# A head's exponentials laid together in DRAM: rows read back in pieces of 2048 bytes instead of four of 512

## The chip, the core and the metric

The kernel runs on one core of a Trainium2 chip. The core has a matrix engine (TensorE, PE in the profile; its weight loads are PEld), three engines for elementwise work (VectorE or DVE, ScalarE or ACT, GpSimd or POOL), and a queue that issues DMAs (SyncE, SP). They run side by side and wait for one another through semaphores. DMAs issued by SP run on the core's 16 DMA engines. The metric is the device time of one execution in microseconds; the median of the runs counts.

## What is computed

There are 64 graphs of 256 nodes with 512 features. Each goes through two layers, the first with two graph attentions. A graph attention projects the features, makes two logits per node and head, and weighs neighbours by a softmax over the sum of the logits of the two ends. Cut to its core, the reference is:

```python
def gat_layer(x, mask, W, a_src, a_dst, bias, concat):
    xl = (x @ W).reshape(B, N, H, F)
    asrc = jnp.einsum('bnhf,hf->bnh', xl, a_src)
    adst = jnp.einsum('bnhf,hf->bnh', xl, a_dst)
    e = jax.nn.leaky_relu(asrc[:, :, None, :] + adst[:, None, :, :], 0.2)
    e = jnp.where(mask[..., None], e, NEG_INF)
    attn = jax.nn.softmax(e, axis=1)
    out = jnp.einsum('bsdh,bshf->bdhf', attn, xl)
    return out + bias                 # concatenated over heads, or their mean

h = relu(layernorm(x))
x = x + gat(elu(gat(h, 4 heads of 256)), 1 head of 512)
h = relu(layernorm(x))
x = x + relu(attention of 8 heads of 64 over h, softmax along the other axis)
```

The attention weights are thus a 256 x 256 matrix for each of 4 + 1 + 8 = 13 heads of a graph. An entry is the exponential of a leaky rectifier of a sum, so it can be had from exponentials of the single logits: apart from a factor that the softmax divides away, it is a maximum of two values, one of which is a product of a node's value and the other node's.

## The kernel before

**Work of a head.** Nodes stand on 128 partitions in T = 2 halves. `exps` (L284 and L481) makes exponentials of the logits for all nodes. One of them, w, is needed as a row: all 256 values of a head, on every partition. `spread` (from L233) does this by way of DRAM. A vector transpose (L237) turns the 128 x 32 tile w, whose columns are (head, half), in blocks of 32 x 32; after it, partition 32 j + c holds the values of column c for the 32 nodes of block j. A DMA (L239) writes this 128 x 32 tile, 16 KB, to `kept` in DRAM. Then one DMA for two heads (L244) reads `kept` back to all 128 partitions at once, into `bc`. Each such read waits for the landing of the write. The columns of two heads lie side by side in a block, so that a partition's row comes as four pieces, one for each block j, of 128 floats (512 bytes); for the single head of the second attention they are 256 bytes. `bc` is thus ordered (block, column, node in block), and `rows` holds views of it, one for each head, in the order (half, block, node in block).

`weigh` (L286 to L290) makes 128 x 256 entries of the weights: ACT multiplies the row by a per-partition value (L289, tile wy), and DVE takes the maximum with another per-partition value and applies the mask (L290, tile e). TensorE then uses e as weights: gat1 (L394), gat2 (L448), gat3 (L500).

**Calls of spread.** `rows1` (4 heads, two reads), `rows2` (1 head, one read) and `rows3` (8 heads, four reads) stand in the step lists. For the last graph rows2 and rows3 are left out, and `spread_at_once` makes the rows with TensorE (L253) in PSUM. `bc2` has four buffers, `bc1` one.

**The projections** are products by blocks with seven multiplications for eight (class Product, L54), whose sums of operands POOL makes (`left`, L215 to L218) and whose results ACT (`kept`, L60) and DVE (`put`, L260) take from PSUM.

**Another tile through DRAM.** The normalised features h of the next graph are written to DRAM and read back rearranged (`away`, L203 and L204), 512 KB each way, and transposed by DVE (`back`, L209) before POOL makes the sums.

**Order.** The whole program is unrolled, in an order written by hand: a head for the first graphs, `order` repeated for each r from 1 to 63, and a tail. Each item of these lists issues its instructions on all engines, and each engine works through its own in order. In `order`, work on three successive graphs is interleaved: the second layer's last attention of graph r-2, the second and third attention of r-1, the first of r, and the first projection of r+1. In one round the row reads come as follows: `1 away1`, later `-1 rows3`, `0 rows2`, then `1 rows1` near the end, followed by `-1 edges3 6` and two products. The next round begins with the last `edges3` and gat3 of r-2 and with edges2; then come edges1 0 and edges1 1, which are the first users of the rows of rows1. On SP, after rows1's reads, follow the two transposing DMAs of `cap3` (L373), the load of the next graph's x and adjacency (L301 and L303), the store of an output (L517), and the next write and read of h.

Of the kernel before, what the change touches and what calls it, by code (L numbers as in the profile page):

```python
# [8 lines left out]
F32 = mybir.dt.float32  # L9
BF16 = mybir.dt.bfloat16  # L10
I32 = mybir.dt.int32
AF = mybir.ActivationFunctionType
# [5 lines left out]
P = 128  # L18
# [14 lines left out]
def rows_of(ap: bass.AP, n: int) -> bass.AP:  # L33

    return bass.AP(tensor=ap.tensor, offset=ap.offset, ap=[[0, P], [1, n]])
# [62 lines left out]
def short_path(ctx, tc, flags, x, adj, w1, att_src1, att_dst1, b1, w2, att_src2, att_dst2, b2, w_proj, w_att,  # L98
               b_att, out):

    nc = tc.nc
    B, N, D = x.shape
# [5 lines left out]
    T = N // P  # L108
# [8 lines left out]
    work = ctx.enter_context(tc.tile_pool(name="work", bufs=2))  # L117
    small = ctx.enter_context(tc.tile_pool(name="small", bufs=4))
    dram = ctx.enter_context(tc.tile_pool(name="dram", bufs=4, space=DRAM))
# [113 lines left out]
    def spread(w, heads):  # L233


        wt = small.tile([P, 32], F32, name="wt")
        nc.vector.transpose(wt, w)  # L237
        kept = dram.tile([4, 32, 32], F32, name=f"kept{heads}")
        nc.sync.dma_start(kept.rearrange("j c i -> (j c) i"), wt)  # L239
        rows = []  # L240
        for h in range(0, heads, 2):
            k = min(2, heads)
            bc = work.tile([P, 4, T * k, 32], F32, name=f"bc{k}", bufs=3 * k - 2)
            nc.sync.dma_start(bc.rearrange("p j c i -> p j (c i)"),  # L244
                              kept[:, T * h:T * (h + k), :].rearrange("j c i -> j (c i)")[None].to_broadcast([P, 4, 32 * T * k]))
            rows += [bc[:, :, T * i:T * (i + 1), :].rearrange("p j t i -> p t j i") for i in range(k)]
        return rows

    def spread_at_once(w, h):

        pm = ps_mm.tile([P, 512], F32, name="pm")
        for t in range(T):
            nc.tensor.matmul(pm[:, t * P:(t + 1) * P], w[:, h, t:t + 1].to_broadcast([P, P]), ident, start=True, stop=True)  # L253
        return pm[:, :N].rearrange("p (t j i) -> p t j i", t=T, j=4)

    def total(dst, pm, add):
        if add is None:
# [28 lines left out]
    def weigh(dst, bc, xw, yw, mask, op):  # L286

        wy = work.tile([P, N], F32, name="wy", bufs=3)
        nc.scalar.activation(wy.rearrange("p (t j i) -> p t j i", t=T, j=4), bc, AF.Copy, scale=yw)  # L289
        nc.vector.scalar_tensor_tensor(dst, wy, xw, mask, ALU.max, op)  # L290

    class Graph:
# [87 lines left out]
        def rows1(self):  # L380
            self.bc1 = spread(self.w[0], H1)

        def edges1(self, h):
            e = self.e[1, h] = work.tile([P, T, N], F32, name="e", bufs=9)
            for s in range(T):
                weigh(e[:, s, :], self.bc1[h], self.ex1[:, h, s:s + 1], self.ex1[:, H1 + h, s:s + 1],
                      self.mask[:, s, :], ALU.mult)
# [42 lines left out]
        def rows2(self):  # L430
            self.bc2 = None if self.b == B - 1 else spread(self.w[1], 1)

        def edges2(self):
            e = self.e[2] = work.tile([P, T, N], F32, name="e", bufs=9)
            bc = self.bc2[0] if self.bc2 else spread_at_once(self.w[1][:, :T].rearrange("p (h t) -> p h t", t=T), 0)
            for s in range(T):
                weigh(e[:, s, :], bc, self.ex2[:, 0, s:s + 1], self.ex2[:, 1, s:s + 1],
                      self.mask[:, s, :], ALU.mult)
# [44 lines left out]
        def rows3(self):  # L483
            self.bc3 = None if self.b == B - 1 else spread(self.w[2], H3)

        def edges3(self, h):
            e = self.e[3, h] = work.tile([P, T, N], F32, name="e", bufs=9)
            bc = self.bc3[h] if self.bc3 else spread_at_once(self.w3, h)
            for s in range(T):
                weigh(e[:, s, :], bc, self.ex3[:, 0, h, s:s + 1], self.ex3[:, 1, h, s:s + 1],  # L490
                      self.cap[:, s, :], ALU.min)
# [20 lines left out]
        def range(self):  # L512
            nc.vector.tensor_reduce(ends[:, 0, self.b:self.b + 1], self.exs, AX.X, ALU.max)
            nc.vector.tensor_reduce(ends[:, 1, self.b:self.b + 1], self.exs, AX.X, ALU.min)
# [434 lines left out]
```

## Time and profile before

| what | value |
|---|---|
| median of 3 runs | 3214.87 us (3212.22 to 3218.14) |
| profiled execution, its own time | 3217.47 us |
| span of the profiled execution, first to last instruction | 3215.8 us |
| mean granted TensorE clock | 0.993 |
| packets of all DMAs | 439,843, 281.49 MB |
| row reads bc<-kept of two heads | 380 of 256 KB, 5.6 us median from issue to landing |
| row reads bc<-kept of one head | 63 of 128 KB, 4.8 us |
| writes kept<-wt | 190 of 16 KB, 1.4 us |
| write of h, read of h | 63 each of 512 KB, 3.2 and 3.6 us |
| DMA queue q1 (all DMAs of SP) | 31.8% of 16 engines' span |
| ACT, L289, wy<-bc | 1646 recorded, 498 ns each |
| ACT's idle time that ended with a landing of bc | 115.5 us in 50 waits |

How to read it: shares of busy time are of the whole span, and a busy matmul is not proof that TensorE is at its peak, because the ends of matmuls are modelled. A bracket at the end of a timeline line gives the idle time of that engine ahead of the group and what ended it. An engine's wait costs something only if the engine that sets the end comes to wait for it. In the stretches, each row holds the length, the busy time of PE, PEld, DVE, ACT and POOL with the number of instructions, then the granted clock, the DMA engines' busy share and the GB/s.

### The profile page before, as it was taken

To read this page: it belongs to the slowest core of one execution; us is meant where nothing else is said; L and a number is where in the kernel's file an instruction comes from. 1 tells how busy PE (TensorE), PEld (TensorE's weight loads), DVE (VectorE), ACT (ScalarE), POOL (GpSimd) and SP (SyncE) were. 2 spreads that over 40 slices of the span, in tenths; PEclk is the share of its full clock that TensorE was granted. 3 is DMA by queue.
4 is the path that set the end of the run, shared out by engine and by line. 5 is a ranking of instruction groups with operands and counts; after the bars stand their busy time and mean duration, and the time that the engine had idled before them with its cause. 6 is when DMAs were issued, how large, how long until landed. Compare 5 with 4: busy or idle time off the path is not lost. (4 is left out here: it accounts for less than half of the span.)

```text
span 3215.8 us, 60905 instructions
## 1 busy us (share of the span) xinstructions
PE 3136.3 (98%) x21808; PEld 2677.7 (83%) x21808; DVE 2285.2 (71%) x6379; ACT 1917.8 (60%) x4867; POOL 1178.1 (37%) x1434
## 2 busy tenths in 40 slices
PE   5899999999999999999999999999999999999997
PEld 3788888888888888888888888888888888888886
DVE  7667677677677677676676776776776776776765
ACT  2456556656666665665565566566566666655654
POOL 2343343343433433433433433434434334334332
PEclk8999999999999999999999999999999999999999
DMA  4233333333333333333333333332333333333331
GB/s 143 57 94 84 90 88 89 84 90 87 88 90 89 88 86 85 96 80 90 97 81 89 88 91 84 91 93 82 92 87 89 88 92 88 84 86 96 81 90 35
DMA packets 439843, 281.49 MB, mean 88 GB/s; under 512 B 109169, under 2 KB 389745, under 8 KB 439537
## 3 DMA queue, kind: packets, MB, share of 16 engines
q1 hardware_dynamic: 438160, 275.43, 31.8%
q8 instruction: 177, 2.90, 0.4%
q10 hardware_dynamic: 1376, 2.10, 0.2%
q14 instruction: 130, 1.06, 0.1%
HBM read 199.36 MB, written 69.70 MB: 84 GB/s over the span
## 5 line engine op out<-in xcount | busy, mean ns | idle before, releaser
L289 ACT ACTIVATE wy<-bc,exs_sb 128x256 f32<-128x256 f32 x1646 | 706.8, 498 | 168.3 <-DMA bc<-kept 115.5
L260 DVE TENSOR_TENSOR xl<-pm,kept 128x256 f32<-128x256 f32 (+2 forms) x768 | 321.7, 419 | 285.8 <-PE pm L54 206.8
L510 POOL TENSOR_TENSOR x<-x,o 128x256 f32<-128x256 f32 x256 | 180.9, 728 | 916.8 <-DVE r L506 885.6
L290 DVE SCALAR_TENSOR_TENSOR e<-wy,exs_sb,cap 128x256 f32<-128x256 f32 x1024 | 435.9, 478 | 92.1 <-ACT wy L289 92.1
L394 PE MATMUL pm<-xl,e 128*128 128x257 f32 x2048 | 488.5, 386 | 12.1 <-DVE e L290 9.1
L54 PE MATMUL sum<-w_sb,h1s 128*128 128x257 f32 x2048 | 489.2, 381 | 5.9 <-POOL h1s L216 3.4
L60 ACT ACTIVATE kept<-sum 128x264 f32<-128x264 f32 (+3 forms) x768 | 276.5, 376 | 338.2 <-PE sum L54 333.1
L54 PEld LDWEIGHTS sum<-w_sb,h1s 128*128 128x128 f32 x2048 | 389.9, 191 | 64.6 <-POOL h1s L216 3.8
L394 PEld LDWEIGHTS pm<-xl,e 128*128 128x128 f32 x2048 | 374.6, 190 | 76.5 <-issue 11.2
L54 PE MATMUL pm<-w_sb,h1s 128*128 128x257 f32 x1536 | 372.2, 385 | 14.9 <-DVE xl L260 10.7
L54 PEld LDWEIGHTS pm<-w_sb,h1s 128*128 128x128 f32 x1536 | 287.9, 191 | 79.4 <-POOL hs L216 21.2
L181 POOL TENSOR_TENSOR rstd<-ve,neg_half 128x2 f32<-128x2 f32 x128 | 117.7, 919 | 636.8 <-DVE ve L179 636.8
L500 PEld LDWEIGHTS pm<-xl,e 128*64 128x64 f32 x8192 | 250.5, 138 | 45.2 <-DVE e L290 23.6
L54 PE MATMUL sum<-w1a_sb,hs 128*128 128x260 f32 x1024 | 270.5, 387 | 11.5 <-ACT kept L60 4.9
L54 PE MATMUL sum<-w1b_sb,hs 128*128 128x256 f32 x1024 | 271.6, 388 | 4.1 <-DVE w1b_sb L536 2.1
L290 DVE SCALAR_TENSOR_TENSOR e<-wy,exs_sb,mask 128x256 f32<-128x256 f32 x640 | 270.3, 481 | 6.3 <-ACT wy L289 6.1
L54 PE MATMUL sum<-wp_sb,hs 128*128 128x264 f32 x1024 | 271.2, 388 | 1.1 <-ACT kept L60 1.1
L500 PE MATMUL pm<-xl,e 128*64 128x65 f32 x8192 | 269.6, 224 | 2.0 <-DVE e L290 1.3
L407 ACT ACTIVATE ez<-z 128x512 f32<-128x512 f32 x256 | 159.6, 624 | 178.2 <-DVE z L404 178.2
L404 DVE SCALAR_TENSOR_TENSOR z<-pm,r,b_sb 128x256 f32<-128x256 f32 x512 | 247.8, 484 | 18.3
L448 PE MATMUL pm<-xl,e 128*128 128x257 f32 (+1 forms) x1024 | 243.7, 381 | 1.0 <-DVE e L290 1.0
L54 PEld LDWEIGHTS sum<-w1a_sb,hs 128*128 128x128 f32 x1024 | 192.4, 191 | 49.4 <-issue 14.3
(99 smaller groups left out, 5025.0 us busy)
## 6 DMA issues: line engine op xcount, KB each, us to landing
bc<-kept SPq DMA_DIRECT2D x380, 256.0 KB, 5.6
xs<-in_x_dram SPq DMA_DIRECT2D x64, 512.0 KB, 4.0
out_dram<-x SPq DMA_DIRECT2D x64, 512.0 KB, 2.8
kept_h<-h SPq DMA_DIRECT2D x63, 512.0 KB, 3.2
h<-kept_h SPq DMA_DIRECT2D x63, 512.0 KB, 3.6
ad<-in_adj_dram SPq DMA_DIRECT2D x64, 256.0 KB, 4.3
bc<-kept SPq DMA_DIRECT2D x63, 128.0 KB, 4.8
kept<-wt SPq DMA_DIRECT2D x190, 16.0 KB, 1.4
```

Of the source, the lines that this page charges most:

```text
L54: self.nc.tensor.matmul(to[:, :self.n], self.lhs[:, i, c, :], self.rhs[:, i, c, :], start=(first and c == 0), stop=(last and c == self.nk ...
L60: self.nc.scalar.activation(s[:, :self.n], self.sum[:, :self.n], AF.Copy)
L181: nc.gpsimd.tensor_tensor(rstd, ve[:, 0, :], neg_half, ALU.pow)
L260: nc.vector.tensor_tensor(dst, pm, add, ALU.add)
L289: nc.scalar.activation(wy.rearrange("p (t j i) -> p t j i", t=T, j=4), bc, AF.Copy, scale=yw)
L290: nc.vector.scalar_tensor_tensor(dst, wy, xw, mask, ALU.max, op)
L394: nc.tensor.matmul(pm[:, :Q + 1], self.e[1, h][:, s, t * P:(t + 1) * P], xl1[:, s, h, L1:], start=(s == 0), stop=(s == T - 1))
L404: nc.vector.scalar_tensor_tensor(z[:, sl], pm[:, :Q], r, b1_sb[:, sl], ALU.mult, ALU.add)
L407: nc.scalar.activation(ez, z[:, 2 * g * F1:2 * (g + 1) * F1], AF.Relu, scale=-1.0)
L448: nc.tensor.matmul(pm[:, :n], self.e[2][:, s, t * P:(t + 1) * P], xl2[:, s, half, L2:L2 + n], start=(s == 0), stop=(s == T - 1))
L500: nc.tensor.matmul(pv[q:q + 64, h, :], self.e[3, a * G + h][:, s, t * P + q:t * P + q + 64], xl3[:, s, a * G + h, :], start=(s == 0), stop ...
L510: nc.gpsimd.tensor_tensor(to, to, o.rearrange("p h k -> p (h k)"), ALU.add)
```

## The change

`kept` is stored with the column ahead of the block, so that all 256 values of a head, and the 512 of two heads, are contiguous in DRAM. The write scatters the 128 pieces of 128 bytes accordingly: its destination is described as 4 x 32 x 32 with strides, where it was a contiguous 128 x 32. The read takes one contiguous piece of 2048 bytes for each partition (1024 bytes for the single head) through `rows_of`, which describes a DRAM range repeated for 128 partitions. `bc` is then in the order of the nodes, and ACT reads a contiguous row in `weigh`, and writes it as before. The number and order of instructions on PE, DVE, ACT and POOL stay the same; on SP the same DMAs are issued in the same order, in other shapes.

```diff
         wt = small.tile([P, 32], F32, name="wt")
         nc.vector.transpose(wt, w)
-        kept = dram.tile([4, 32, 32], F32, name=f"kept{heads}")
-        nc.sync.dma_start(kept.rearrange("j c i -> (j c) i"), wt)
+        kept = dram.tile([32, 4, 32], F32, name=f"kept{heads}")
+        nc.sync.dma_start(kept.rearrange("c j i -> j c i"), wt)
         rows = []
         for h in range(0, heads, 2):
             k = min(2, heads)
-            bc = work.tile([P, 4, T * k, 32], F32, name=f"bc{k}", bufs=3 * k - 2)
-            nc.sync.dma_start(bc.rearrange("p j c i -> p j (c i)"),
-                              kept[:, T * h:T * (h + k), :].rearrange("j c i -> j (c i)")[None].to_broadcast([P, 4, 32 * T * k]))
-            rows += [bc[:, :, T * i:T * (i + 1), :].rearrange("p j t i -> p t j i") for i in range(k)]
+            bc = work.tile([P, k, N], F32, name=f"bc{k}", bufs=3 * k - 2)
+            nc.sync.dma_start(bc.rearrange("p h n -> p (h n)"),
+                              rows_of(kept[T * h:T * (h + k)].rearrange("(h t) j i -> h (t j i)", t=T), k * N))
+            rows += [bc[:, i] for i in range(k)]
         return rows
...
-        return pm[:, :N].rearrange("p (t j i) -> p t j i", t=T, j=4)
+        return pm[:, :N]
...
-        nc.scalar.activation(wy.rearrange("p (t j i) -> p t j i", t=T, j=4), bc, AF.Copy, scale=yw)
+        nc.scalar.activation(wy, bc, AF.Copy, scale=yw)
```

with the helper that the new read calls:

```python
def rows_of(ap: bass.AP, n: int) -> bass.AP:
    return bass.AP(tensor=ap.tensor, offset=ap.offset, ap=[[0, P], [1, n]])
```

## The prediction

> **What bounds the kernel now.** I read the page first (busy shares, slices), then busy time by stretches, then what TensorE waits for, then the timelines around the row reads that the change touches.
>
> ```profile
> PE 3136.3 (98%) x21808; PEld 2677.7 (83%) x21808; DVE 2285.2 (71%) x6379; ACT 1917.8 (60%) x4867; POOL 1178.1 (37%) x1434
> PE   5899999999999999999999999999999999999997
> ...
> kept<-wt SPq DMA_DIRECT2D x190, 16.0 KB, 1.4
> ```
>
> ```profile
> 0.00:60.00 60.00, 27.58 (x83) 20.27 (x84) 48.18 (x180) 14.77 (x32) 13.15 (x22) 0.86 0.56 173
> 60.00:120.00 60.00, 45.79 (x184) 36.53 (x183) 36.45 (x85) 21.73 (x51) 20.75 (x26) 0.89 0.16 45
> ...
> 1170.00:2170.00 1000.00, 995.19 (x7028) 852.48 (x7027) 721.69 (x2004) 615.64 (x1564) 367.20 (x446) 1.00 0.33 88
> ```
>
> The first column after the stretch's length is PE's busy time: 995.2 of 1000 us in the steady state. Busy PE is not proof of peak, so I took the period as well: from the first L448 matmul of a graph to that of the next, the 62 full distances have a lowest and median value of 48.57 us. Their sum exceeds 62 x 48.57 by 12.9 us. That is all a steady-state repair can win unless it shortens PE's own work, and the change leaves every matmul as it is.
>
> What are the 12.9 us? TensorE's waits between 170 and 3120 us:
>
> ```profile
> PE pm L54 <- DVE xl L260: 5.3, 35, 0.2
> PE sum L54 <- ACT kept L60: 3.9, 11, 0.5
> PE pm L394 <- DVE r L402: 1.5, 4, 0.4
> PE pm L394 <- DVE r L506: 1.3, 5, 0.3
> ```
>
> No DMA is named, so I looked graph by graph at which distance is long. Seven long ones, 4.5 us together, have the L394 waits; fourteen, 7.5 us, wait late in the period where the first layer's product needs the returned h (L203/L204), and in these the h write took 4.5 to 4.9 us instead of 3.2. The first distance is 0.4 too long and one other 0.4. The seven belong to the row reads. A normal graph (2541 us) beside one of the seven (2784 us): SP's issues and ACT, then DVE and PE.
>
> ```profile
> 2541.07 0.33 SPq L239 DMA_DIRECT2D kept<-wt  x1
> 2542.56 0.91 SPq L244 DMA_DIRECT2D bc<-kept  x2
> ...
> 2547.65 1.30 ACT L289 ACTIVATE wy<-bc,exs_sb 128x256 f32<-128x256 f32 x3 [1.97 <-DMA bc<-kept]
> ...
> 2784.72 0.33 SPq L239 DMA_DIRECT2D kept<-wt  x1
> 2786.22 0.91 SPq L244 DMA_DIRECT2D bc<-kept  x2
> ...
> 2792.66 1.70 ACT L289 ACTIVATE wy<-bc,exs_sb 128x256 f32<-128x256 f32 x4 [3.33 <-DMA bc<-kept]
> ```
>
> ```profile
> 2548.38 0.39 DVE L260 TENSOR_TENSOR xl<-pm,kept 128x256 f32<-128x256 f32 x1
> 2548.69 1.66 DVE L290 SCALAR_TENSOR_TENSOR e<-wy,exs_sb,mask 128x256 f32<-128x256 f32 x4
> ...
> 2793.20 1.68 DVE L290 SCALAR_TENSOR_TENSOR e<-wy,exs_sb,mask 128x256 f32<-128x256 f32 x4 [0.78 <-ACT wy L289]
> ...
> 2798.20 1.97 PE L394 MATMUL pm<-xl,e 128*128 128x257 f32 x8 [0.34 <-DVE r L402]
> 2800.43 1.97 PE L394 MATMUL pm<-xl,e 128*128 128x257 f32 x8 [0.26 <-DVE r L506]
> ```
>
> ACT waits for the row read in both. In the normal graph that costs nothing: DVE reaches the edge weights at 2548.69 straight from other work (no idle bracket), with the first wy already there. In the late graph DVE idles 0.78 us, everything behind it on DVE slips, and PE finds its PSUM buffers not yet emptied. In all seven the loss fits one rule: a microsecond lost for each microsecond by which the first row read of rows1 lands later than 7.03 us after the issue of its write (7.95 us landed, 0.92 lost; 8.13, 1.10; 7.59, 0.55; 7.30, 0.27). Landing times over the 62 later graphs have a median of 6.6 us: slack is 0.4 us.
>
> **What the skill says.** The Trainium skill, "DMA: Bandwidth & Descriptors", section "Why a DMA increments its semaphore by 16 and not by 1": the number k of DMA engines is the largest up to 16 that divides the slowest dimension of both sides. The write's destination was 128 x 32 and becomes 4 x 32 x 32, so k falls from 16 to 4; the reads keep 128 partitions. No trace of before shows a k below 16 here. The same page, "Specifications", puts line rate at 512 B and more. The trace disagrees for these reads: 512-byte packets of bc take 27 ns when queued densely, yet a lone pair of reads starts 160 packets per us for its first 2 us, and the lone 256-byte reads (rows2) run at about 150 per us throughout, while the h write of 512-byte pieces runs at 560 per us. The small reads look limited by count, not bytes. The Trainium skill, "Runtime: NRT & Kernel Launch", "Instruction fetch mechanics": instructions come in blocks of 16 KiB over DMA. The trace agrees (177 packets, 2.90 MB on the instruction queue, about 1 us each); such blocks fall into the h write in most of the fourteen late graphs.
>
> **The change part by part.** The times that follow are from one issue to its landing.
>
> 1. *Write (L239), 190 times.* Still 128 pieces of 128 bytes, at 13 ns each in the trace. On 16 engines 8 each, on 4 engines 32 each: 24 x 13 = 0.31 us longer, 1.42 becomes 1.73. Low end: 1.42, if nothing changes. High end: if 32 pieces in a row on one engine go at the slow pace of the reads (16 engines at 170 per us, 94 ns a piece), 24 x 94 = 2.3 us longer, 3.7. I take 1.73, since the writes were seen at 13 ns.
>
> 2. *Read (L244), 443 times.* 128 packets of 2048 bytes instead of 512 of 512 (rows2: 128 of 1024 instead of 512 of 256). The nearest row is h<-kept_h, DRAM to SBUF in 2048-byte packets, 256 of them, landing in 3.6 us; its dense phase runs at 192 packets per us, so 128 fewer save 0.67: 3.0 us. Median for the first read of rows1 now: 5.05. Low end 2.5 (half of h's whole active time of 2.2 us saved), high end 5.05 (no gain, as all partitions read the same 2 KB). I take 3.0.
>
> 3. *Sum for rows1.* Now 1.48 (write and SP's wake-up) + 5.05 = 6.5 us; after it 1.8 + 3.0 = 4.8, some 1.7 us earlier. That is 2.2 us ahead of 7.03, more than any late case lacked (1.10), so all seven losses go: -4.5 us. What is late next in those graphs is DVE, which is then back to back as at 2548.69, and behind it PE itself; the other graphs gain nothing, as their statistics and h writes start at the same offsets (16.9 and 21.9 us into the period) whether the row landed 6.1 or 7.0 us after the issue.
>
> 4. *rows3 and rows2.* ACT's waits for bc belong to rows1: no gain. Behind the waiting reads on SP stand the next write, the cap transposes, and the loads; SP waits for far later things (wt, x2), so a shorter or 0.3 us longer write is hidden. If a write became 2.3 us longer, the reads' own shortening would repay most of it.
>
> 5. *ACT reading contiguous rows (L289).* The strided read takes 498 ns; L321, 256 contiguous elements of SBUF with a per-partition operand, takes 500. I expect 498 again. A saving of up to 90 ns would be hidden, as PE is the bound.
>
> 6. *Head and tail.* Graph 0 has the largest PE wait (9.1 us for e), and its row lands at 51.5 us. But DVE is busy without a break until 52.80, where the first e starts, and the wy is ready by 52.1: no gain. In graph 1 DVE idles 0.28 us before e: -0.3 us. The last graph's rows2 and rows3 come from TensorE: nothing.
>
> Sum: -4.5 - 0.3 = -4.8 us against the profiled execution's own 3217.47 (span 3215.8 and 1.7 around it): 3212.7. That execution lies 2.6 above the median 3214.87, near the top of the runs (3212.22 to 3218.14), so a median run may have a little less to lose. Taken from the median: 3210.1. I predict 3210.
>
> **Rivals.**
> - *The gain is larger:* shorter row traffic also frees the DMA engines, so that half of the late-h excess (7.5 + 0.4) goes too: -4.8 - 4 = about 3206. For it: bc is the largest share of packets (some 227,000 of 439,843). Against it: h's write does not overlap bc in time, and its lateness comes from instruction blocks whose place the change doesn't move.
> - *The reads don't get faster* (a shared row, not the count, limits them): write +0.31, read as now. Shifting all 62 landing times by this and applying the rule gives a loss of 10.3 instead of the 4.7 that it gives for now: +5.6, about 3220.5. Against it: the 256-byte reads have the same count pace as the 512-byte ones, which no limit in bytes explains.
> - *Slower: the write on four engines eats the slack.* If it costs 2.3 us more and the read gains only 1, rows1 lands 1.3 us later than now; by the rule some 62 us are lost (1.3 us in nearly every graph, less the slack) instead of 4.7: +57, about 3272. It decides from +0.4 us net (12.5 instead of 4.7 lost, 0.24%). Against it: 13 ns a piece.
>
> **How the numbers follow.** Forecast 0.61, its own range 3206 to 3214; larger gain 0.22; reads no faster 0.09; slower by the write 0.08. About 0.2%, 6.4 us, is what a measurement of this kernel tells from no change: the bounds are 3208.4 and 3221.3. The forecast lies 4.8 below the median, so a third of it (0.20) falls under 3208.4: faster 0.20 + 0.22 = 0.42. Slower: 0.08 and 0.01 of the unchanged reads, 0.09. Same: 0.49. The 80% range takes in the larger gain and most of the unchanged reads: 3204 to 3218.
>
> **What would show it.** Some 170,000 packets fewer (443 reads x 384), so about 270,000 in all; bc landing in 3 us; the write near 1.7; ACT's wait for bc nearly gone; no L394 wait for r in the steady state; the shortest period still 48.57; the late-h distances still there. I'd be wrong in mechanism if the shortest period moved, if the write landed after more than 3 us, or if the late-h losses vanished as well.

## The result, and the profile after

The changed kernel takes 3209.32 us (median of 20 runs, 3206.74 to 3210.77), the kernel before, run on the same chip, 3214.65 us (20 runs, 3208.38 to 3218.66). The ratio is 0.9984, with a 95% interval of 0.9977 to 0.999: 5.3 us less, and small beside the 10 us over which single runs of before scatter. The changed kernel also scatters less, 4 us.

The page of the changed kernel, by its busy shares, its packets and its issues by size:

```profile
PE 3132.0 (98%) x21808; PEld 2678.1 (83%) x21808; DVE 2283.9 (71%) x6379; ACT 1919.6 (60%) x4867; POOL 1178.1 (37%) x1434
...
DMA packets 267450, 281.48 MB, mean 88 GB/s; under 512 B 74632, under 2 KB 168712, under 8 KB 267144
...
L289 ACT ACTIVATE wy<-bc,exs_sb 128x256 f32<-128x256 f32 x1646 | 708.4, 498 | 155.9 <-DVE e L290 92.2
...
L290 DVE SCALAR_TENSOR_TENSOR e<-wy,exs_sb,mask 128x256 f32<-128x256 f32 x640 | 270.2, 480 | 1.7 <-ACT wy L289 1.7
```

172,000 packets are gone, and not one engine's busy time has moved by more than 5 us. ACT takes 498 ns for a row's product with a contiguous operand, as it did with a strided one. What has moved is waiting: DVE's idle time ahead of the masked weights (last line) fell to 1.7 us. Before, the same line was:

```profile
L290 DVE SCALAR_TENSOR_TENSOR e<-wy,exs_sb,mask 128x256 f32<-128x256 f32 x640 | 270.3, 481 | 6.3 <-ACT wy L289 6.1
```

ACT's own wait for the rows fell from 115.5 us to 49.7 (49 waits), less than half, but it is not nearly gone, which was one of the prediction's signs. In return ACT waits longer for DVE to take its results (the end of the L289 line: 92.2 us, 23.6 before).

TensorE's waits in the steady state, 170 to 3115 us, all that are listed:

```profile
PE pm L54 <- DVE xl L260: 5.0, 33, 0.2
PE sum L54 <- ACT kept L60: 3.7, 10, 0.5
PE pm L54 <- POOL hs L217: 0.6, 4, 0.2
PE pm L54 <- POOL hs L216: 0.3, 2, 0.2
```

Both L394 waits, for r of L402 and of L506, are absent. The others stand as they were.

One normal graph, in the timelines of SP, ACT and DVE:

```profile
2535.08 0.52 SPq L239 DMA_DIRECT2D kept<-wt  x1
2537.08 0.80 SPq L244 DMA_DIRECT2D bc<-kept  x2
```

```profile
2540.77 1.31 ACT L289 ACTIVATE wy<-bc,exs_sb 128x256 f32<-128x256 f32 x3 [1.07 <-DMA bc<-kept]
```

```profile
2542.39 0.39 DVE L260 TENSOR_TENSOR xl<-pm,kept 128x256 f32<-128x256 f32 x1
2542.70 1.66 DVE L290 SCALAR_TENSOR_TENSOR e<-wy,exs_sb,mask 128x256 f32<-128x256 f32 x4
```

From the issue of the write to that of the first read 2.00 us now pass, where there were 1.49 in the graph shown of before; ACT starts on the row 5.69 us after the write's issue, where it was 6.58. DVE begins the weights 7.62 us after the write's issue, as it did before, right behind its previous work: being early by most of a microsecond has bought nothing in this graph. Over the 62 later graphs ACT's start has a median of 5.58 and a maximum of 6.15 us (before 6.70 and 8.22).

The page gives no times of landing for the changed kernel, but they can be had from the semaphore updates that the trace keeps, because a DMA reports its end by raising a semaphore, and has landed with the last update of its own (SP issues the read that waits for a write 0.05 us after it). Before, every DMA has 16 of them (17,648 in all). The changed kernel has 15,558, which is 11 fewer for each of the 190 scattered writes: these have five. In medians over the 62 later graphs, in us, for the write of rows1 and its first read:

| | before | changed |
|---|---|---|
| write, issue to first packet | 0.83 | 1.16 |
| write, first packet's start to last packet's end | 0.23 | 0.37 |
| write, issue to landing | 1.41 | 1.92 |
| read, issue to landing | 5.06 | 3.52 |
| both, from the write's issue to the read's landing | 6.61 | 5.50 |

The distances between the first L448 matmuls of successive graphs tell where the time went. The lowest is 48.56 and the median 48.57, as before. The excess of the 62 full distances over 62 x 48.57 us is 7.3 us instead of 12.9. The seven long distances that belonged to late rows (4.5 us) are at the floor, the first distance lost 0.3 of its 0.4, and the late-h ones stand, at some 6.8 us where they were 7.5. The two profiled spans differ by 8.1 us (3215.8 and 3207.7), 2.5 more than these 5.6. Some 1.3 of this lies before the first rows are even written (their write stands at 43.8 us instead of 45.1), so it is not the change's; in the profiles of this study the first L448 matmul comes anywhere between 104.2 and 106.7 us. About 1.0 lies behind the last full distance, and its cause is open.

### The profile page after: what moved, and what is told of

It is laid out like the page before. It is cut to its first block, busy times and chain, and to the rows that moved or that the text cites. A ratio compares the mean times of both kernels' runs of the same rounds, so it can differ in the third digit from the quotient of the medians.

```text
span 3207.7 us, 60905 instructions
## 1 busy us (share of the span) xinstructions
PE 3132.0 (98%) x21808; PEld 2678.1 (83%) x21808; DVE 2283.9 (71%) x6379; ACT 1919.6 (60%) x4867; POOL 1178.1 (37%) x1434
## 3 DMA queue, kind: packets, MB, share of 16 engines
q14 instruction: 129, 1.06, 0.1%
## 5 line engine op out<-in xcount | busy, mean ns | idle before, releaser
L289 ACT ACTIVATE wy<-bc,exs_sb 128x256 f32<-128x256 f32 x1646 | 708.4, 498 | 155.9 <-DVE e L290 92.2
L510 POOL TENSOR_TENSOR x<-x,o 128x256 f32<-128x256 f32 x256 | 181.0, 728 | 922.0 <-DVE r L506 890.4
L394 PE MATMUL pm<-xl,e 128*128 128x257 f32 x2048 | 486.6, 386 | 9.1 <-DVE e L290 9.1
L394 PEld LDWEIGHTS pm<-xl,e 128*128 128x128 f32 x2048 | 374.9, 190 | 70.8 <-issue 12.1
L448 PE MATMUL pm<-xl,e 128*128 128x257 f32 (+1 forms) x1024 | 242.8, 380 | 1.0 <-DVE e L290 1.0
```

The lines of the kernel that those rows point to most:

```text
L289: nc.scalar.activation(wy, bc, AF.Copy, scale=yw)
L394: nc.tensor.matmul(pm[:, :Q + 1], self.e[1, h][:, s, t * P:(t + 1) * P], xl1[:, s, h, L1:], start=(s == 0), stop=(s == T - 1))
L448: nc.tensor.matmul(pm[:, :n], self.e[2][:, s, t * P:(t + 1) * P], xl2[:, s, half, L2:L2 + n], start=(s == 0), stop=(s == T - 1))
L510: nc.gpsimd.tensor_tensor(to, to, o.rearrange("p h k -> p (h k)"), ALU.add)
```

## Experiments

Each kernel was timed in rounds with the kernel before on the same chip.

**The two halves of the change, and the two groups of rows.** Four kernels ran together, on one chip. The two halves leave out the reordering that goes with them: their rows hold the values in another order than the weights need, while their instructions and DMAs are otherwise those of the kernel that each starts from.

Write alone: the kernel before with the scattered write; the reads keep their four pieces.

```diff
-        kept = dram.tile([4, 32, 32], F32, name=f"kept{heads}")
-        nc.sync.dma_start(kept.rearrange("j c i -> (j c) i"), wt)
+        kept = dram.tile([32, 4, 32], F32, name=f"kept{heads}")
+        nc.sync.dma_start(kept.rearrange("c j i -> j c i"), wt)
+        kept = kept.rearrange("c j i -> (c j) i").rearrange("(j c) i -> j c i", j=4)
```

> The write scatters to four engines as in the changed kernel, the reads keep their four pieces of 512 bytes; the reads take their four pieces from where they stood before, so the rows hold the values in another order, and the weights are made of these. Theory (only the landing of the first row read of rows1 counts; a microsecond beyond 7.03 us after the issue of its write costs a microsecond in that graph): the write lands 0.5 us later (SP issues the first read 1.94 us after the write in the changed kernel, 1.43 before), so the read lands at about 7.1 in the median graph; shifting the 62 landings of before by 0.5 gives 15.8 us of losses instead of 4.7, so +11 us, ratio 1.0034 (1.002 to 1.005), with an L394 wait in some half of the graphs. Rival (fewer packets on the DMA engines are what gains): as many packets as before, so ratio 1.000 within 0.001.

Read alone: the changed kernel with the contiguous write; the reads take one piece.

```diff
-        kept = dram.tile([32, 4, 32], F32, name=f"kept{heads}")
-        nc.sync.dma_start(kept.rearrange("c j i -> j c i"), wt)
+        kept = dram.tile([4, 32, 32], F32, name=f"kept{heads}")
+        nc.sync.dma_start(kept.rearrange("j c i -> (j c) i"), wt)
+        kept = kept.rearrange("j c i -> (j c) i").rearrange("(c j) i -> c j i", j=4)
```

> The write is the contiguous one of before, the reads take one piece of 2048 bytes; the pieces are contiguous where they stood before, so the rows hold other values. Theory: the first read of rows1 lands at about 5.0 us after the issue of the write, earlier than in the changed kernel (5.5), but both are far ahead of 7.03, so the time is that of the changed kernel: -4.7 us, ratio 0.9985 (0.9975 to 0.9995). Rival (the landing itself shifts something further, so earlier is better at any time): some more than the changed kernel, ratio 0.997 or less.

The whole change for rows1 alone, set into the kernel before (for rows2 and rows3 alone, the condition is `heads != H1`):

```diff
+        if heads == H1:
+            kept = dram.tile([32, 4, 32], F32, name=f"kept{heads}")
+            nc.sync.dma_start(kept.rearrange("c j i -> j c i"), wt)
...
+            return rows
         kept = dram.tile([4, 32, 32], F32, name=f"kept{heads}")
```

> The whole change for the four heads of the first attention alone (126 of 443 reads). Theory: the whole gain, -4.7 us, ratio 0.9985 (0.9975 to 0.9995), no L394 wait for r in the steady state. Rival (fewer packets): 126 of the 443 reads, a gain of 1.5 us, ratio 0.9995.

> The whole change for rows2 and rows3 alone, rows1 as before. Theory: no gain, ratio 1.000 within 0.001, the L394 waits for r in some seven graphs as before. Rival (fewer packets): 317 of the 443 reads, a gain of 3.7 us, ratio 0.9988.

| kernel | median us (runs) | ratio to before, 95% interval | ACT's start on the row: median, maximum |
|---|---|---|---|
| before | 3212.77 (65) | | 6.70, 8.22 |
| write alone | 3215.66 (13) | 1.001, 1.0002 to 1.0018 | 6.96, 7.56 |
| read alone | 3209.52 (21) | 0.9987, 0.9981 to 0.9994 | 4.94, 6.51 |
| rows1 alone | 3208.84 (21) | 0.9989, 0.9983 to 0.9996 | 5.54, 7.13 |
| rows2 and rows3 alone | 3211.97 (21) | 0.9995, 0.9988 to 1.0001 | 6.55, 8.94 |

The last column is of one profiled execution each, in us from the issue of the rows1 write; for before it is the profile read by the prediction.

The write half by itself costs time, the read half gives back more. Read alone has its rows 0.6 us earlier than the change for rows1 alone and is no faster than it, as far as the intervals tell: once the rows are ahead of their deadline, more earliness buys nothing. The rows of rows1, 126 of 443 reads, carry the gain. For rows2 and rows3, which are 317 reads, the interval reaches from a gain of 0.12% to a loss of 0.01%; a share of the gain in proportion to packets (0.9988) lies at its very end, and the profile of that kernel shows the row losses still there: 2.0 us in five waits of the first attention's matmuls, L394 before, L406 here. So packets as such are not what gained, though a few tenths of a microsecond from the other rows are not excluded.

The write alone was a miss in size: 11 us expected, about 3 measured. SP's part came as supposed:

```profile
2537.09 0.52 SPq L239 DMA_DIRECT2D kept<-wt  x1
2539.08 0.91 SPq L245 DMA_DIRECT2D bc<-kept  x2
```

This is SP's timeline of the write-alone kernel, where L245 is the read: 1.99 us from write to read, 0.5 more than before. But ACT's start moved by only 0.26 in the median, because the four-piece reads landed 4.89 us after their issue, where it was 5.06 before. Most of that is not the write's doing: in the profile of rows2 and rows3 alone, whose rows1 is that of before and which ran on the same chip, they took 4.95. And the forecast had shifted the tail of before along with the rest. That tail was in part late writes: the contiguous write of rows1 landed up to 3.08 us after its issue before, and up to 2.58 in the profile of rows2 and rows3 alone; the 62 scattered ones of this profile all landed between 1.91 and 1.95. So the latest start (7.56) is earlier than before's, and the rule, put to the landings of this profile, gives 3.1 us, less than it gives for before. This profile is the fastest of the kernel's 13 runs and no fair sample; where the 2.9 us of the medians arise is not shown.

**Later by one DMA.** The changed kernel with the rows of rows1 copied once more within DRAM.

```diff
         nc.sync.dma_start(kept.rearrange("c j i -> j c i"), wt)
+        if heads == H1:
+            again = dram.tile([32, 4, 32], F32, name="again")
+            nc.sync.dma_start(again.rearrange("c j i -> (c j) i"), kept.rearrange("c j i -> (c j) i"))
+            kept = again
```

> The changed kernel, with the rows of rows1 copied once more from DRAM to DRAM before they are read, so that they land later by one DMA (about 2.2 us, some 7.7 us after the issue of the write; 5.5 in the changed kernel). Theory (beyond 7.03 us a microsecond costs a microsecond, in each graph): 0.6 to 0.7 us in each of 62 graphs, +41 us over the changed kernel, about +36 over before: ratio 1.011 (1.005 to 1.02), the median distance between graphs no longer 48.57 but about 49.2. Rival (the seven losses were collisions of another kind, and lateness by itself is absorbed by slack elsewhere): median distance still 48.57, ratio below 1.002.

Measured: 3257.36 us (4 runs), ratio 1.0135, 1.0119 to 1.015; +43.5 us over before. TensorE's timeline of that kernel, in a graph like those shown (L398 is the first attention's matmul, L406 and L510 the reciprocals):

```profile
2042.89 1.97 PE L398 MATMUL pm<-xl,e 128*128 128x257 f32 x8 [0.44 <-DVE r L406]
2045.12 1.97 PE L398 MATMUL pm<-xl,e 128*128 128x257 f32 x8 [0.26 <-DVE r L510]
```

They are the same two waits as in the late graphs of before, now in most graphs. Between 170 and 3110 us TensorE has, beside 11 waits for e (5.8 us in all):

```profile
PE pm L398 <- DVE r L510: 12.2, 49, 0.3
PE pm L398 <- DVE r L406: 9.6, 25, 0.4
```

ACT's start has a median of 7.71 and a maximum of 9.55 us, and the median distance between graphs rose to 49.35 us. The rule applied to the landings of this profile (all later than 7.03 us) gives 48.3 us; the excess of its 62 distances is 54.3. So most of the excess is lateness beyond the deadline, one for one, and the rest is that of h (see the last table of this section). The expectation had put the median lateness into every graph, and the long tail made the mean larger.

**The other deadline.** The changed kernel with the way of h split by t.

```diff
-        nc.sync.dma_start(kept.rearrange("t a p e -> p t a e"), h.rearrange("p t (a e) -> p t a e", a=4))
-        nc.sync.dma_start(h, kept.rearrange("t a (j q) e -> (a j) t (q e)", q=4))
+        for t in range(T):
+            nc.sync.dma_start(kept[t].rearrange("a p e -> p a e"), h[:, t].rearrange("p (a e) -> p a e", a=4))
+        for t in range(T):
+            nc.sync.dma_start(h[:, t], kept[t].rearrange("a (j q) e -> (a j) (q e)", q=4))
```

> The changed kernel, with the way of h through DRAM split by t: two writes of 256 KB, then two reads of 256 KB, each waiting for its own half alone. Theory (the losses that the changed kernel still has in the steady state, 7.3 us in its profile, come from h landing late when the write meets other DMA traffic, and h has some 0.8 us of slack at most): the second half lands about 1.2 us earlier than h does now, the fourteen or so late graphs vanish for the most part, -5 to -6 us below the changed kernel: ratio to before 0.9968 (0.996 to 0.998). Rival (two more DMAs with their own fixed cost bring the end of the second half no earlier): as the changed kernel, 0.9985, or some 0.9995 if it lands later.

Measured: 3202.09 us (5 runs), ratio 0.9961, 0.9947 to 0.9974. This version is faster than before (by 11.8 us), and its interval lies wholly below that of the changed kernel (0.9977 to 0.999). Its SP queue, and TensorE's waits between 170 and 3110 us, which are all that is listed:

```profile
2021.12 1.18 SPq L204 DMA_DIRECT2D kept_h<-h  x2
2023.79 1.34 SPq L206 DMA_DIRECT2D h<-kept_h  x2
```

```profile
PE pm L54 <- POOL hs L219: 7.1, 47, 0.2
PE pm L54 <- DVE xl L262: 0.2, 1, 0.2
```

The first read of h is issued 2.67 us after the first write, which is the longest of the 62 later graphs (median 2.39); in the changed kernel the median was 3.25 and the longest 4.93. The last read now lands 6.21 us after the first write's issue in the median and 8.00 at the latest, where it was 6.91 and 8.80: 0.7 to 0.8 us earlier, not the 1.2 of the expectation, and just enough, as the next table shows. In the place of ten waits of up to 0.5 us for `kept`, a new small one stands, for POOL's sums. It comes in 47 graphs at 0.15 us each, but the median distance stays at 48.57, so it seems to take the place of a wait that was there (33 for xl). The excess over the 62 distances is 0.6 us: the steady state is at its floor.

**Are the two deadlines separate?** The same split of h, with the rows as before.

> The kernel before, with only the way of h in two halves; rows as before. Theory (two separate deadlines in a graph, each with its own losses): the losses by late h go (7 us), those by late rows stay (some 4 to 5 us in a run), so ratio 0.9978 (0.997 to 0.9988), L394 waits for r in a handful of graphs still there, excess over 62 x 48.57 us of 4 to 6 us. Rival (one kind of loss hides behind the other, or the gain of the halves needs the lighter row traffic): ratio 0.999 or more, or all of the excess gone.

Measured: 3205.53 us (7 runs), ratio 0.9971, 0.996 to 0.9983. TensorE's waits between 170 and 3110 us:

```profile
PE pm L54 <- POOL hs L219: 7.6, 50, 0.2
PE pm L396 <- DVE r L404: 1.3, 3, 0.4
PE pm L396 <- DVE r L508: 1.0, 4, 0.3
```

The waits for h are gone and those for the rows stay. The excess is 5.0 us, of which 4.1 stand in eight graphs in which the rule gives 4.2. The two losses add up: 0.9971 and 0.9984 multiply to 0.9955, and 0.9961 was measured for both. The halves alone gained more in these runs (9.4 us) than the 7 us that the profile of before held for late h.

**Both deadlines, graph by graph.** In the late graphs of the changed kernel a second rule can be read, of the same kind: h's last landing against 7.95 us after the issue of its write (8.80 us landed, 0.84 lost; 8.44, 0.50; 8.22, 0.28). With the two limits held fixed, the lateness of rows1 and of h was summed over the graphs of every profile, in us:

| kernel | excess | rows1 beyond 7.03 | h beyond 7.95 | left over |
|---|---|---|---|---|
| before | 12.9 | 4.9 | 7.4 | 0.5 |
| changed | 7.3 | 0 | 6.9 | 0.4 |
| write alone | 9.5 | 3.1 | 5.7 | 0.8 |
| read alone | 7.3 | 0 | 6.7 | 0.6 |
| rows1 alone | 7.2 | 0 | 6.6 | 0.6 |
| rows2 and rows3 alone | 10.9 | 3.3 | 7.2 | 0.5 |
| extra hop | 54.3 | 48.3 | 5.9 | 0.1 |
| h in halves | 0.6 | 0 | 0.1 | 0.5 |
| halves alone | 5.0 | 4.3 | 0.1 | 0.6 |

The two add up within single graphs too: in each profile at least 58 of the 62 distances come out within 0.05 us. The rows of a graph count in the distance after the one in which they are written; where h is in halves, its last half counts. In every profile one graph has about 0.35 us more, for a cause that stays open.

## Why the prediction was right

- *The bound and what can be won.* TensorE's floor of 48.57 us in a graph held in every profile but the one with the extra hop (48.64 at the lowest there). The excess was the right place to look.
- *The deadline.* The rule of one microsecond per microsecond beyond 7.03 us, read from seven graphs, gave 48.3 of the 54.3 us of excess when the extra hop moved all graphs beyond it, the rest being late h, and 4.2 for 4.1 where rows stayed as they were. This is shown by runs. That DVE is the engine on which slack ends is read from the timelines only.
- *The sum.* -4.5 for the seven graphs and -0.3 for graph 1 became -4.5 and -0.3 in the profile. The -5.3 us of the medians agree with the -4.8 no better than their interval allows, some -7.4 to -3.2 us, so the closeness of 3209.32 to 3210 is in part luck.
- *Step 1, the write,* was short: 0.31 us more supposed, 0.51 measured. That four engines take part is what the trace shows (last section). But the working had only the longer stream of packets, which grew by 0.14 and not by 0.31. It had left out that the first packet starts 0.33 us later; 0.19 of this is SP's own issue, which grew from 332 to 522 ns. The write landed at 1.92 us, far from the 3 us that would have refuted the mechanism.
- *Step 2, the read,* was short as well: 3.0 us supposed, 3.38 measured behind the contiguous write (read alone) and 3.52 in the whole change. The working had taken the pace from h's dense phase, 192 packets per us; in the first 2 us the row reads start 106 and 97 per us. So rows1 gained 1.1 us in the median and not 1.7, and ACT still waits for its rows. It didn't matter, as the latest row of the profile still came 0.96 us ahead of the limit: both steps were short, the row landed at 5.50 us where the sum had 4.8, and the room before the deadline took it up.
- *Steps 4 to 6:* no measurable change from rows2 and rows3, 498 ns on ACT, and the head without gain (TensorE's wait for e in graph 0 is 9.1 us in both profiles, although ACT's start on its row came 1.06 us sooner after the write's issue).
- *The rivals.* The larger gain fell: the late-h losses stayed, 7.5 and about 6.8 us. The read did get faster. The slower one is borne out in its sign alone: the write without the read is slower than before by 0.1%.

Two things make the result less sharp than it reads. The gain lies within the scatter of single runs of before; only the interval over twenty runs of each kernel parts them. And the number of late rows is a draw: with the same rows1, 11 of the 62 rows landed beyond 7.03 us in the profile of before, five in that of rows2 and rows3 alone, and eight in that of the halves alone.

## What to carry to other kernels

In a kernel that is 99.5% busy on its bound, measure the period of the steady state and sort what lies above its floor by deadline; each deadline has its own slack, and only what lands beyond it costs anything. A faster transfer is worth the lateness of its tail, here 0.1 us in a graph on average, and not the microsecond that it saves. When one deadline has been met with room to spare, look for the next (here h), rather than make the first transfer still faster.

## What was not expected of the hardware

- The first row read of rows1, 256 KB to 128 partitions from the same 2 KB of DRAM, landed 3.38 us after its issue in one piece of 2048 bytes for each partition behind the contiguous write, and 3.45 and 3.52 behind the scattered one (rows1 alone and the whole change). In four pieces of 512 bytes it took 4.89 to 5.10 in four profiles.
- A pair of these reads starts at about 80 packets per us in its first 0.7 us, half of the 160 to 170 per us at which the 512-byte ones started; so the pace at the start is neither a fixed count nor a fixed number of bytes. What sets it is open.
- The issue of a DMA whose destination is 4 x 32 x 32 kept SP for 522 ns, that of the contiguous 128 x 32 for 332 (320 in the profile of read alone). The Trainium skill, "DMA: Bandwidth & Descriptors", section "Why a DMA increments its semaphore by 16 and not by 1", says that the issuing sequencer itself adds the remaining 16 - k of the count. The trace agrees, with k = 4: in a graph of the changed kernel the five updates of the scattered write come 0.94, 1.88, 1.89, 1.90 and 1.92 us after its issue. The first of them precedes the first packet (1.16 us), so no finished piece can have made it; the other four come behind the last packet.
- A 16 KB packet of the instruction queue, about 1 us long, was in flight in each of the 109 writes of h that landed more than 4 us after their issue in the seven profiles with undivided h, and in three of the 332 others, which took at most 3.7 us. No run moves these packets, so that they are the cause of the lateness is argued, not shown.
